# The last group's transition matrix: built transposed, row sums as columns, base blocks put down by TensorE

## The chip, the cores and the metric

One core of one Trainium2 chip. The metric is device microseconds of one execution of the program, the median of 3 runs.

## The reference

128 batches, each with 128 nodes and 512 features, and an adjacency of 128 x 128. Two graph layers, each followed by a residual and a layer norm over the features; cut to what matters:

```python
# layer 0
deg = jnp.sum(adj, axis=-1, keepdims=True)
agg = jnp.einsum('bij,bjf->bif', adj, x) / jnp.maximum(deg, EPS)
x = layernorm(x + relu(jnp.concatenate([x, agg], axis=2) @ W.T))
# layer 1
Xw = X @ Wv + bv
sj = Xw @ aw[:d, 0]
si = Xw @ aw[d:, 0]
e = leaky_relu(sj[:, None, :] + si[:, :, None] + ab[0], negative_slope=0.2)
alpha_matrix = A * jnp.exp(e)
transition = alpha_matrix / (jnp.sum(alpha_matrix, axis=-1, keepdims=True) + 1e-12)
for k in range(3):
    H = H + Xk @ Wk[k] + bk[k]
    Xk = jnp.einsum('bij,bjd->bid', transition, Xk)
x = layernorm(x + relu(H))
```

The part that the change touches is `transition` of the last four batches, and how the sum over k is then put together for them.

## The kernel before

The batches go in 32 groups of four (`G = 4`, `NG = 32`), through layer 0 first and then through layer 1. All numbers are float32; a product is two passes of TensorE. The weight products are done block by block with seven products instead of eight, at two levels. In layer 1 an outer block is one of O1 to O7 (`outer`), each made of seven products of 385 columns, O1.1 to O1.7. Four times 385 columns hold, in this order, X W2, X W1, X W0, two columns for the scores si and sj, and two of padding. So the sum of the reference is taken from the inside, T(T(X W2) + X W1) + X W0 plus biases.

`combine` does that, in eight products of 512 columns (c.1 to c.8; x.1 to x.8 for the last group). For each of the four batches b, `one(b)` multiplies the transition matrix with X W2 into a PSUM bank, VectorE adds X W1 to give `v1`, and ScalarE then copies the base, X W0, into the same bank (`row(b, 254, 766, 1)`). `two(b)` multiplies the transition matrix with `v1` and adds it to what stands in the bank. `residual` follows on VectorE.

The transition matrix comes as follows. `t_scores` takes the score columns out of two of the O results. For all groups but the last, sj goes through memory to be spread over the partitions, the matrix is normed, stored, and loaded back in blocks of 32 (`load_blocks`, by `swap_in`), which VectorE's 32 x 32 transpose then turns (`t_turn`), since TensorE wants it transposed. Most of that lies beside the next group's products. The last group has no next one. There, `t_scores` makes four diagonal matrices of sj (`dg`), and a product with ones spreads them over the partitions (`t_exp`). ScalarE adds si in a leaky ReLU (Prelu) and takes Exp. GpSimd multiplies with the adjacency, VectorE sums the rows and takes the reciprocal (`t_sums`). ScalarE scales the rows, four products with the identity turn the matrix, and ScalarE copies the four results out of PSUM (`t_norm`).

Two lanes of four PSUM banks each (bA0 to bA3, bB0 to bB3) carry the products of two outer blocks side by side. In the last group O4 and the combine stand in lane 1 (bA); lane 0 (bB) is done after O3. At the program's start one identity product is written into each of the eight banks.

The order of the work is written out by hand. `PL` is the order of TensorE's products in the last group, and `PLACES_L` and `PLACES_M` say at which place in it every other operation is issued (`PLACES_M` those of the group before, "group 30", whose layer norm falls into this stage; the last is group 31). Each engine runs its instructions in the order of issue. SyncE issues the transfers, also in order. `late` holds residuals and evictions that are issued right after a product. `need` only checks the order while the program is built.

The names that the steps of the prediction use: c is the combine of group 30; the "early" addition is GpSimd's at L667, the O3.5 addition VectorE's at L670, evictions with an addition L663; L255, L784 are VectorE's transposes; L471 and L967 are additions at the start; L500 is the square whose sum gives the variance; "apply" is the last step of a layer norm (`ln_apply`, `end_apply`); w2row is a small matrix at the start that is turned by products of two columns.

Of the kernel before, what the change touches and what calls it, by code (L numbers as in the profile page):

```python
# [16 lines left out]
def kernel(  # L17
# [15 lines left out]
    P = 128  # L33
# [63 lines left out]
    def load_adj(n):  # L97
        g = n % NG
        adjs[n] = p1.tile([P, G, N], FP, name="ag")
        nc.sync.dma_start(adjs[n], adj[g * G : (g + 1) * G].rearrange("b i j -> i b j"))  # L100
# [46 lines left out]
    for t in bA + bB:  # L147
        nc.tensor.matmul(t, ident, ident[:, None, :].to_broadcast([P, Q, P]), start=True, stop=True)
# [566 lines left out]
    def t_scores(g):  # L715
        need(("O3", g, 7), ("sum_c", g, 0), ("sum_c", g, 1))
        si = small.tile([P, G], FP, name="si")
        for p, t in ((0, rs[NG + g]), (1, last22[g])):
            L_.copy(sj[:, 2 * p : 2 * p + 2], t[:, :, 1, 381])
            L_.activation(si[:, 2 * p : 2 * p + 2], t[:, :, 1, 382], AF.Identity, bias=cc)  # L720
        if g == NG - 1:
            dg = p1.tile([P, G, N], FP, name="dg", tag="sb")
            for b in range(G):
                V.tensor_scalar(dg[:, b], ident, sj[:, b : b + 1], None, ALU.mult)
            Ts[g] = dg, si
            return
        turned = small.tile([P, R], FP, name="turned")
        V.transpose(turned, sj)
        d = dram.tile([R, Q, R], FP, name="scd")
        nc.sync.dma_start(d.rearrange("b q r -> q b r"), turned)  # L730
        Ts[g] = d, si

# [8 lines left out]
    def t_exp(g):  # L741
        need(("t_load", g) if g < NG - 1 else ("t_scores", g))
        T, si = Ts[g]
        if g == NG - 1:
            dg, T = T, p1.tile([P, G, N], FP, name="T", tag="aT")
            pt = lanes[0][0]
            mm(pt, ones[:].to_broadcast([P, P]), dg, True)
        for b in range(G):
            src = T[:, b] if g < NG - 1 else pt[:, b * N : (b + 1) * N]
            L_.activation(T[:, b], src, AF.Prelu, bias=si[:, b : b + 1], alpha=SLOPE)  # L750
        Ts[g] = T, si
        L_.activation(T, T, AF.Exp)
# [12 lines left out]
    def t_norm(g):  # L765
        need(("t_sums", g))
        T, rr = Ts[g]
        for b in range(G):
            L_.activation(T[:, b], T[:, b], AF.Copy, scale=rr[:, b : b + 1])
        if g < NG - 1:  # L770
            swap_out(NG + g, T)
            return
        TTs[g] = p1.tile([P, G, N], FP, name="TT")
        for b in range(G):
            pt = lanes[0][1 + b // 2]
            mm(pt[:, b % 2 * N : (b % 2 + 1) * N], T[:, b], ident, b % 2 == 0)
            L_.copy(TTs[g][:, b], pt[:, b % 2 * N : (b % 2 + 1) * N])
# [8 lines left out]
    def combine(lane, g):  # L786
        n = NG + g
        X, Y, W, Z = lane
        at_ = {0: X, 1: Z, 2: W, 3: Y}
# [8 lines left out]
        def one(b):  # L798
            need(("O4" if b > 1 else "O3", g, 7), ("sum_c", g, 0), ("sum_c", g, 1))
# [4 lines left out]
            L_.copy(at_[b], row(b, 254, 766, 1))  # L804

        def two(b):
            mm(at_[b], TTs[g][:, b], v1[b])
            late.append((residual, n, b, at_[b]))
# [15 lines left out]
    def step(lane, name, g, k):  # L824
# [11 lines left out]
    PL = ("o3.7 O1.1 O1.2 O2.1 O1.3 O2.2 O1.4 O1.5 O1.6 O1.7 O2.3 O2.4 O5.1 O2.5 O2.6 O5.2 O2.7 O5.3 O5.4 O6.1 O5.5 O5.6 "  # L836
          "O6.2 O5.7 O6.3 O7.1 O6.4 O6.5 O7.2 O7.3 O7.4 O6.6 O7.5 O6.7 O7.6 O7.7 O3.1 O3.2 O3.3 O3.4 c.1 c.2 c.3 c.4 "
          "O3.5 c.5 c.6 c.7 c.8 O4.1 O3.6 O4.2 O3.7 O4.3 O4.4 O4.5 O4.6 O4.7 x.1 x.2 x.3 x.4 x.5 x.6 x.7 x.8").split()
# [42 lines left out]
    def place_op(n, pos, name, m, *a):  # L881
# [3 lines left out]
        else:  # L885
# [37 lines left out]
        ("ln_mean",): 213, ("ln_var", 1): 224, ("ln_scales",): 226, ("ln_var", 2): 222, ("ln_apply", 0): 234,  # L923
        ("ln_apply", 3): 237, ("ln_apply", 1): 230, ("y_store", 1): 255, ("ln_var", 0): 224, ("y_store", 0): 243,
        ("ln_var", 3): 213, ("ln_apply", 2): 242,
    }
    PLACES_L = {
        ("end_store", 2): 150, ("t_norm",): 115, ("sum_r", 0): 71, ("end_store", 0): 153, ("t_scores",): 105,
        ("sum_r", 1): 71, ("t_exp",): 107, ("end_apply", 0): 147, ("load_adj",): 96, ("end_apply", 1): 152,
        ("load_y", 1): 94, ("end_store", 1): 163, ("t_sums",): 111, ("end_stats", 3): 137, ("end_mean", 0): 125,  # L930
        ("end_apply", 2): 139, ("end_var", 1): 131, ("end_mean", 1): 130, ("end_stats", 2): 130, ("end_rstd", 2): 132,
        ("load_y", 0): 57, ("end_store", 3): 155, ("end_apply", 3): 151, ("end_scales",): 133, ("end_var", 0): 125,
        ("sum_c", 0): 76, ("end_rstd", 3): 145, ("sum_c", 1): 76,
    }
    OPS = {f.__name__: f for f in (load_left, load_y, load_adj, x_turn, x_inner, x_s1, x_s2, x_s3, x_s4, sum_c22, degree, a_norm, a_load, a_turn, w_slot, ln_mean, ln_var, ln_scales, ln_apply, y_store, sum_r, sum_c, t_scores, t_load,
           t_exp, t_sums, t_norm, t_back, t_turn)}
    ENDS = {f.__name__: f for f in (end_mean, end_var, end_scales, end_stats, end_rstd, end_apply, end_store)}
    LAST = {"ln_mean", "ln_var", "ln_scales", "ln_apply", "y_store"}
    OWN = {"sum_r", "sum_c", "t_scores", "t_load", "t_exp", "t_sums", "t_norm", "t_back", "t_turn"}
# [112 lines left out]
```

## Time and profile before

| | |
|---|---|
| median of 3 runs | 2092.91 us (2092.64 to 2092.97) |
| the profiled execution | 2093.66 us |
| its span, first to last instruction | 2091.9 us |
| mean granted clock of TensorE | 0.998 |
| TensorE products | 2074.7 us, 99% |
| VectorE, ScalarE, GpSimd | 70%, 55%, 73% |

The span is what the trace shows; 1.76 us of the profiled execution lie around it. A time such as 2066.00 is counted from the span's start. In a timeline the first number is the start, the second the duration, then come engine, line, operation, what is written from what, the count, and in brackets how long the engine was idle before it and what ended that. SPq is SyncE's queue. Rows that follow each other are merged.

### The profile page before, as it was taken

The page shows a single profiled execution, that of the slowest core. Times are in us where ns is not written, and L with a number is a line of the kernel's source. Part 1 is how long each engine was busy: PE and PEld are TensorE (multiplying, and loading weights), DVE is VectorE, ACT ScalarE, POOL GpSimd, SP SyncE. Part 2 cuts the span into 40 slices and gives each one's busy share as a digit, 9 for nine tenths or more (in the row PEclk, how much of TensorE's full clock was granted, in tenths as well). Part 3 has the DMA queues.
Part 4 walks back from the last instruction along what each step waited for, and adds up shares of the span by engine and source line. Part 5 has one row for each costly group of instructions (what it writes and reads, how often), then busy time and mean ns, then how long its engine had stood idle before and what let it go on. Part 6 is the DMA issues. An engine that isn't in the chain of part 4 may idle for free.

```text
span 2091.9 us, 25884 instructions
## 1 busy us (share of the span) xinstructions
PE 2074.7 (99%) x7100; PEld 1330.3 (64%) x7100; DVE 1465.5 (70%) x3247; ACT 1153.7 (55%) x2883; POOL 1532.2 (73%) x1424
## 2 busy tenths in 40 slices
PE   9999999999999999999999999999999999999997
PEld 6778888888778886555555555555555555555553
DVE  6777777777777777666666666666666666666665
ACT  2656666666666666355455455455455455455454
POOL 5777888887767776867767767767767767767763
PEclk9999999999999999999999999999999999999999
DMA  9777766676667767335534434534534534534523
GB/s 207 171 189 194 180 178 178 161 190 194 158 165 190 188 171 237 87 86 122 115 87 122 115 86 122 115 86 122 115 86 124 114 86 124 113 87 122 115 66 116
DMA packets 429486, 287.13 MB, mean 137 GB/s; under 512 B 153497, under 2 KB 352281, under 8 KB 429340
## 3 DMA queue, kind: packets, MB, share of 16 engines
q1 hardware_dynamic: 428412, 284.15, 53.7%
q10 hardware_dynamic: 800, 1.31, 0.3%
q8 instruction: 56, 0.92, 0.2%
q14 instruction: 90, 0.74, 0.1%
q0 software_dynamic: 128, 0.01, 0.0%
HBM read 191.60 MB, written 93.79 MB: 136 GB/s over the span
## 4 chain that ended last, share of the span: by engine, by line
PE 96%; DMA 1%; POOL 1%; DVE 1%; ACT 0%; issue 0%; ACTq 0%; DVEq 0%; POOLq 0%
PE bA L151 50%; PE bB L151 45%; DMA big<-in_w0t_dram 1%; DMA yd<-y 0%; DMA xb<-in_x_dram 0%; DMA y<-in_x_dram 0%; PE bA L177 0%; POOL s L667 0%; POOL c L711 0%; POOL r L703 0%; ACT junk L500 0%; DVE y L376 0%; POOL xs L266 0%; POOL xs L270 0%; POOL xu L278 0%
## 5 line engine op out<-in xcount | busy, mean ns | idle before, releaser
L151 PE MATMUL bB<-big,xu 128*128 128x385 f32 (+1 forms) x1806 | 562.1, 434 | 0.7 <-DVE r L670 0.5
L151 PEld LDWEIGHTS bB<-big,xu 128*128 128x128 f32 x1806 | 341.8, 190 | 167.7 <-issue 44.8
L151 PE MATMUL bA<-big,xl 128*128 128x256 f32 (+1 forms) x1358 | 405.8, 416 | 0.4 <-DVE bA L471 0.3
L151 PE MATMUL bB<-big,xs 128*128 128x256 f32 (+1 forms) x1316 | 384.1, 416 | 0.0
L151 PEld LDWEIGHTS bA<-big,xl 128*128 128x128 f32 x1358 | 257.1, 190 | 100.1 <-issue 15.6
L151 PEld LDWEIGHTS bB<-big,xs 128*128 128x128 f32 x1316 | 249.1, 190 | 84.8 <-ACT bB L624 6.2
L151 PE MATMUL bA<-big,xu 128*128 128x256 f32 (+1 forms) x896 | 294.3, 440 | 0.4 <-DVE bA L633 0.2
L667 POOL TENSOR_TENSOR s<-s,r 128x385 f32<-128x385 f32 x128 | 128.1, 1001 | 182.2 <-DVE bB L633 139.1
L151 PE MATMUL bA<-c,TT 128*128 128x512 f32 x512 | 241.3, 593 | 0.0
L500 ACT ACTIVATE junk<-y,mv 128x512 bf16<-128x512 f32 x252 | 182.6, 725 | 89.5 <-POOL mv L495 85.3
L151 PEld LDWEIGHTS bA<-big,xu 128*128 128x128 f32 x896 | 162.0, 189 | 95.4 <-DVE r L657 19.3
L513 ACT ACTIVATE y<-y,mv,rstd 128x512 f32<-128x512 f32 x252 | 202.1, 815 | 0.6 <-POOL mv L508 0.6
L376 DVE SCALAR_TENSOR_TENSOR y<-bA,y 128x512 f32<-128x512 f32 x256 | 170.5, 684 | 23.4 <-PE bA L151 16.9
L151 PE MATMUL bA<-big,xs 128*128 128x385 f32 x448 | 173.7, 499 | 0.0
L151 PE MATMUL bB<-big,xl 128*128 128x385 f32 (+1 forms) x462 | 172.0, 480 | 0.8 <-ACT bA L452 0.4
L633 DVE TENSOR_TENSOR bB<-bB,s 128x385 f32<-128x385 f32 x128 | 72.5, 567 | 121.0 <-PE bB L151 83.2
L151 PEld LDWEIGHTS bA<-c,TT 128*128 128x128 f32 x512 | 97.2, 190 | 89.4 <-issue 48.8
L624 ACT COPY bB<-bB 128x385 f32<-128x385 f32 x128 | 60.1, 470 | 143.8 <-PE bB L151 143.8
L278 POOL TENSOR_TENSOR xu<-xu,xs 128x896 f32<-128x896 f32 x63 | 131.7, 2090 | 8.8 <-PE bB L151 8.8
L274 POOL TENSOR_TENSOR xl<-xu,xl 128x896 f32<-128x896 f32 x63 | 133.5, 2120 | 1.1
L270 POOL TENSOR_TENSOR xs<-xs,xu 128x896 f32<-128x896 f32 x63 | 132.0, 2095 | 2.4
L266 POOL TENSOR_TENSOR xs<-xl 128x896 f32<-128x896 f32 x63 | 131.3, 2085 | 0.0
(182 smaller groups left out, 3474.8 us busy)
## 6 DMA issues: line engine op xcount, KB each, us to landing
xb<-in_x_dram SPq DMA_DIRECT2D x256, 128.0 KB, 3.8
y<-in_x_dram SPq DMA_DIRECT2D x64, 512.0 KB, 4.2
yd<-y SPq DMA_DIRECT2D x64, 512.0 KB, 3.0
xb<-yd SPq DMA_DIRECT2D x256, 128.0 KB, 5.2
y<-yd SPq DMA_DIRECT2D x64, 512.0 KB, 4.6
out_dram<-y SPq DMA_DIRECT2D x62, 512.0 KB, 2.8
ag<-in_adj_dram SPq DMA_DIRECT2D x64, 256.0 KB, 5.1
sb<-sd SPq DMA_DIRECT2D x252, 64.0 KB, 3.2
```

Source lines behind the costliest of these rows:

```text
L151: nc.tensor.matmul(dst, lhsT, rhs, start=start, stop=True, skip_group_check=True)
L266: S_.tensor_add(xs[n][:, 0], xl[n][:, 0], xl[n][:, 1])
L270: S_.tensor_sub(xs[n][:, 1], xs[n][:, 0], xu[n][:, 0])
L274: S_.tensor_sub(xl[n][:, 0], xu[n][:, 0], xl[n][:, 0])
L278: S_.tensor_sub(xu[n][:, 1], xu[n][:, 1], xs[n][:, 1])
L376: V.scalar_tensor_tensor(y, t, 0.0, y, ALU.max, ALU.add, accum_out=mvs[n][:, b, 0:1])
L500: L_.activation(junk, ys[n, b // 2][:, b % 2], AF.Square, bias=mvs[n][:, b, 0:1], accum_out=mvs[n][:, b, 1:2])
L513: L_.activation(y, y, AF.Identity, bias=mvs[n][:, b, 0:1], scale=rstds[n][:, b : b + 1])
L624: L_.copy(Y, X)
L633: V.tensor_add(W, X, s5)
L667: S_.tensor_add(s5, s5, part(src, BZ, BW))
```

## The change

Only the last group and the program's start are changed.

- The matrix is built transposed from the beginning. The diagonals are made of si, and sj is the column that ScalarE adds (`end_scores`); Prelu and Exp go in two halves of two batches. The last group's adjacency is loaded in blocks of 32 and turned by VectorE (`adj_turn`), and VectorE multiplies with it (`end_rows`) in place of GpSimd.
- The row sums are four products with a column of ones, one column each (`end_rows`). VectorE adds epsilon, takes the reciprocal, and makes diagonals of it (`end_recip`). A product with ones spreads these over the partitions, and VectorE multiplies the matrix with that out of PSUM (`end_norm`). The four turning products and their four copies are gone.
- The base of batches 0, 1 and 2 is written by a product with the identity into three banks of lane 0 (`end_base`), and `two(b)` adds to it there. Batch 3 still has its base copied by ScalarE, into bank X.
- `PL`, `PLACES_L` and `PLACES_M` are new: c.5 to c.8 stand together, O4.4 comes before the product that spreads the scores, `sum_c` and O3's early addition change places on GpSimd, the last group's two y loads stand at other places on SyncE, and the last steps of the layer norms have new places.
- The identity product into bank bB3 at the start is left out.

```diff
     def load_adj(n):
         g = n % NG
+        if n == 2 * NG - 1:
+            adjs[n] = p1.tile([P, G, Q, R], FP, name="agb", tag="ag")
+            load_blocks(adjs[n], adj[g * G : (g + 1) * G])
+            return
...
-    for t in bA + bB:
+    for t in bA + bB[:3]:
         nc.tensor.matmul(t, ident, ident[:, None, :].to_broadcast([P, Q, P]), start=True, stop=True)
...
             for b in range(G):
-                V.tensor_scalar(dg[:, b], ident, sj[:, b : b + 1], None, ALU.mult)
+                V.tensor_scalar(dg[:, b], ident, si[:, b : b + 1], None, ALU.mult)
...
+    def adj_turn():
+        need(("load_adj", 2 * NG - 1))
+        src = adjs[2 * NG - 1]
+        adjs[2 * NG - 1] = p1.tile([P, G, N], FP, name="agT", tag="aT")
+        V.transpose(adjs[2 * NG - 1].rearrange("p g n -> p (g n)"), src.rearrange("p g j r -> p (g j r)"))
+
+    def end_scores(g):
+        need(("t_scores", g), ("C", g - 1, 8))
+        (dg, _), pt = Ts[g], lanes[0][0]
+        mm(pt, ones[:].to_broadcast([P, P]), dg, True)
+        T = TTs[g] = p1.tile([P, G, N], FP, name="TT")
+        for b in range(G):
+            L_.activation(T[:, b], pt[:, b * N : (b + 1) * N], AF.Prelu, bias=sj[:, b : b + 1], alpha=SLOPE)
+            if b % 2:
+                L_.activation(T[:, b - 1 : b + 1], T[:, b - 1 : b + 1], AF.Exp)
+
+    def end_rows(g, h):
+        need(("end_scores", g), ("adj_turn",), *[("end_rows", g, 0)] * h)
+        T, pt = TTs[g], lanes[0][0]
+        t2 = T[:, 2 * h : 2 * h + 2].rearrange("p b n -> p (b n)")
+        V.tensor_mul(t2, t2, adjs[2 * NG - 1][:, 2 * h : 2 * h + 2].rearrange("p b n -> p (b n)"))
+        for b in (2 * h, 2 * h + 1):
+            mm(pt[:, b : b + 1], T[:, b], ones, b == 0)
+
+    def end_recip(g, h):
+        need(("end_rows", g, 1))
+        t = lanes[0][0][:, 2 * h : 2 * h + 2]
+        rr = small.tile([P, 2], FP, name="rr2")
+        V.tensor_scalar(rr, t, ROW_EPS, None, ALU.add)
+        V.reciprocal(rr, rr)
+        if h == 0:
+            ends["dr"] = p1.tile([P, G, N], FP, name="dr", tag="sb")
+        for b in (0, 1):
+            V.tensor_scalar(ends["dr"][:, 2 * h + b], ident, rr[:, b : b + 1], None, ALU.mult)
+
+    def end_norm(g, h):
+        need(("end_recip", g, 1), *[("end_norm", g, 0)] * h)
+        T = TTs[g][:, 2 * h : 2 * h + 2].rearrange("p b n -> p (b n)")
+        pt = lanes[0][0][:, h * FH : (h + 1) * FH]
+        mm(pt, ones[:].to_broadcast([P, P]), ends["dr"][:, 2 * h : 2 * h + 2].rearrange("p b n -> p (b n)"), h == 0)
+        V.tensor_mul(T, T, pt)
+
+    def end_base(g, b):
+        need(("sum_c" if b > 1 else "O3", g, 0 if b > 1 else 7))
+        t = (rs[NG + g], last22[g])[b // 2][:, b % 2].rearrange("p n m -> p (n m)")
+        mm(lanes[0][1 + b], ident, t[:, 254:766], True)
...
-        TTs[g] = p1.tile([P, G, N], FP, name="TT")
-        for b in range(G):
-            pt = lanes[0][1 + b // 2]
-            mm(pt[:, b % 2 * N : (b % 2 + 1) * N], T[:, b], ident, b % 2 == 0)
-            L_.copy(TTs[g][:, b], pt[:, b % 2 * N : (b % 2 + 1) * N])
...
-        at_ = {0: X, 1: Z, 2: W, 3: Y}
+        at_ = to = {0: X, 1: Z, 2: W, 3: Y}
+        if g == NG - 1:
+            to = {0: lanes[0][1], 1: lanes[0][2], 2: lanes[0][3], 3: X}
...
-            L_.copy(at_[b], row(b, 254, 766, 1))
+            if g < NG - 1 or b == 3:
+                L_.copy(to[b], row(b, 254, 766, 1))
 
         def two(b):
-            mm(at_[b], TTs[g][:, b], v1[b])
-            late.append((residual, n, b, at_[b]))
+            need(*[("end_base", g, b)] if g == NG - 1 and b < 3 else [])
+            mm(to[b], TTs[g][:, b], v1[b])
+            late.append((residual, n, b, to[b]))
...
     PL = (...)
-          "... O3.1 O3.2 O3.3 O3.4 c.1 c.2 c.3 c.4 "
-          "O3.5 c.5 c.6 c.7 c.8 O4.1 O3.6 O4.2 O3.7 O4.3 O4.4 O4.5 O4.6 O4.7 x.1 x.2 x.3 x.4 x.5 x.6 x.7 x.8")
+          "... O3.1 O3.2 O3.3 O3.4 c.1 c.2 c.3 c.4 "
+          "c.5 c.6 c.7 c.8 O4.1 O3.5 O4.2 O3.6 O3.7 O4.3 O4.4 O4.5 O4.6 O4.7 x.1 x.2 x.3 x.4 x.5 x.6 x.7 x.8")
...
     PLACES_L = {
...
-        ("t_norm",): 115, ("t_scores",): 105, ("t_exp",): 107, ("t_sums",): 111, ("load_adj",): 96, ("load_y", 1): 94, ("load_y", 0): 57,
+        ("t_scores",): 105, ("adj_turn",): 100, ("end_scores",): 108, ("end_base", 2): 110, ("end_base", 0): 111,
+        ("end_rows", 0): 111, ("end_rows", 1): 111, ("end_recip", 0): 111, ("end_recip", 1): 112, ("end_base", 1): 112,
+        ("end_norm", 0): 113, ("end_norm", 1): 115, ("load_adj",): 92, ("load_y", 0): 39, ("load_y", 1): 115,
...
     }
```

In the order of TensorE's queue the end of the changed program is: O4.3, O4.4, the product that spreads the scores, O4.5, base 2, base 0, the four row sums, O4.6, base 1, first norm product, O4.7, second norm product, combine.

## The prediction

> **What bounds the kernel now.** I read the shares of busy time first, then the chain that ended last, then the waits of TensorE, and last the timeline of the two ends.
>
> ```profile
> PE 2074.7 (99%) x7100; PEld 1330.3 (64%) x7100; DVE 1465.5 (70%) x3247; ACT 1153.7 (55%) x2883; POOL 1532.2 (73%) x1424
> ...
> PE 96%; DMA 1%; POOL 1%; DVE 1%; ACT 0%; issue 0%; ACTq 0%; DVEq 0%; POOLq 0%
> ```
>
> TensorE is busy 2074.7 of 2091.9 us: only 17.2 us can be saved without taking a product away. 2.7 of them lie before its first instruction and 8.4 behind its last. The waits of TensorE from 2000 us on show the others:
>
> ```profile
> PE bB L151 <- ACT T L769: 2.2, 1, 2.2
> PE bB L151 <- ACT TT L777: 0.9, 2, 0.5
> PE bB L151 <- DVE dg L724: 0.8, 1, 0.8
> ```
>
> All three are the last group's transition matrix, which nothing covers once the O4 products run out. Its timeline (TensorE alone), and then three two-microsecond stretches (length, busy us and count of PE, PEld, DVE, ACT and POOL, then the granted clock, DMA share, GB/s):
>
> ```profile
> 2054.13 2.74 PE L151 MATMUL bA<-c,TT 128*128 128x512 f32 x6
> ...
> 2066.00 1.12 PE L151 MATMUL bB<-dg,ones 128*128 128x512 f32 x2 [0.79 <-DVE dg L724]
> 2066.97 3.09 PE L151 MATMUL bA<-big,xl 128*128 128x385 f32 x8
> 2072.29 0.49 PE L151 MATMUL bB<-ident,T 128*128 128x128 f32 x2 [2.23 <-ACT T L769]
> ...
> 2075.41 3.46 PE L151 MATMUL bA<-c,TT 128*128 128x512 f32 x6
> ```
>
> ```profile
> 2064.00:2066.00 2.00, 1.22 (x4) 0.38 (x2) 1.39 (x6) 1.01 (x5) 0.00 (x0) 1.00 0.00 0
> ...
> 2074.00:2076.00 2.00, 1.64 (x6) 1.10 (x5) 0.00 (x0) 0.80 (x3) 0.00 (x0) 0.50 0.00 0
> 2076.00:2078.00 2.00, 2.00 (x5) 0.87 (x4) 0.76 (x2) 0.00 (x0) 0.00 (x0) 0.79 0.00 0
> ```
>
> The reader is to see two losses: TensorE waits, and the three products that took 2.74 us in the group before take 3.46 us here, at half the clock. The head of the program:
>
> ```profile
> 2.66 6.52 PE L148 MATMUL bA<-ident 128*128 128x512 f32 x8 [2.66 <-POOL ident masks.py:199]
> ...
> 9.02 3.60 PE L148 MATMUL bB<-ident 128*128 128x512 f32 x8
> ...
> 12.45 3.83 PE L151 MATMUL bA<-big,xu 128*128 128x256 f32 x17
> ```
>
> The eight identity products (two passes each) run until the first real product at 12.45, without a gap. Their weight loads stand 0.85 apart up to 8.6 us and 0.43 after it: the clock is up long before they end.
>
> **The change, part by part.** All times below are on the clock of this trace. A product of 512 columns takes 0.86 us (2.74 for three, less the tail of the last), of 385 columns 0.65.
>
> *One identity product less.* At full clock a product of 512 takes 0.86, so the first real one can start at 11.59. What it reads is there: xu is turned by 9.75, and VectorE uses the same weights at 11.38; their first difference, which the second product needs at 12.45 now, is done at 12.07. The limit is the second x block: VectorE turns it at 15.65 without a wait, its last load was issued at 10.53, and a load on SyncE that waits for this one goes out at 15.43. If it lands only then, the turning moves up by 0.25, the 0.30 us wait behind it (before L471) gives 0.3 more, and the products that follow move by 0.55; if it lands by 14.8, all 0.86 is kept. I take 0.7 (ends 0.5 and 0.86). Behind it TensorE is busy throughout, so a shift reaches the end; the two gaps of the head (0.28 at 26.8, 0.45 at 37) end on VectorE and ScalarE work that moves along.
>
> *The regrouped order of the last group.* The same O1 to O7 products, in another order: 0, at most 0.3 either way (a bubble of one dependent addition). The combine of the group before (c.5 to c.8) now runs without O3.5 between. Its last product waits for VectorE's two additions (0.43, 0.41) and ScalarE's copy (0.59), which start 0.65 earlier like it: 0.1 lost, as now. So O4.3 still ends at 2065.06.
>
> *O4.4 ahead of the broadcast product* fills 0.65 of the 0.79 us wait. The diagonal stays due at 2065.94: VectorE gets the transpose of the adjacency (0.70, row of L784) into the hole between the O3.5 addition (ends 2063.2) and O3.6's, which waits for TensorE until 2063.95. ScalarE has one square ahead of the scores (0.72 and 0.19), and the second pair of si is there at 2065.3, where the third diagonal needs it at 2065.46.
>
> *From the broadcast product to the combine.* Product at 2066.00 to 2066.97. TensorE then goes O4.5 (to 2067.62), base 2 (2068.48), base 0 (2069.34). Beside it ScalarE does two Prelu (from 2067.23, 0.28 apart), Exp of 256 (0.63 for 512 and a copy's 0.47 for 385 against 0.59 for 512: about 0.42), again two and one: 2068.27 and 2069.22. VectorE multiplies 256 columns in 0.42 each (L243): 2068.73 and 2069.68. The four row sums are eight weight loads with one column each; eight such passes (w2row) took from 55.7 to 56.5, so 0.11 each: to 2070.28. Then O4.6 (2070.93), base 1 (2071.79). VectorE meanwhile: plus epsilon 0.18 from 2070.48, reciprocal 0.18, two diagonals (0.28, 0.19 apart; they also wait for a square on ScalarE, whose buffer they take, at 2070.8), O4.6's addition 0.56, the second plus epsilon, which ends at 2071.97. The first norm product must wait for that, since it overwrites the sums: 2072.14, 0.35 idle. It takes 0.43; O4.7 to 2073.22; the second norm waits for VectorE's multiplication of the first half (2072.77 to 2073.20): 2073.37 to 2073.80, 0.15 idle. The combine starts at 2073.80, against 2075.41. Cross-check, O4 products aside: between 2066.97 and 2075.41 stood 5.85 us of waits, transposes and copies; now there are three bases (2.58), two norms (0.86), row sums (0.9) and 0.50 of waits, 4.84; with the 0.65 of O4.4 that is 1.66, against 1.61.
>
> *The combine* is eight products of 0.86 = 6.89, to 2080.68. Before: 2075.41 to 2083.33, which is 7.92. ScalarE's three base copies (0.59 each) are off its path; the fourth is done near 2078.6, due 2079.8. 2.65 us gained at TensorE's end.
>
> *The finish.* VectorE now has apply 2 ahead of the statistics of block 3. Last residual near 2082.3, apply 2 waits for GpSimd's power (0.57) until 2082.63, statistics of block 3 to 2083.98, GpSimd to 2084.88, apply 3 to 2085.46; ScalarE's two applies end at 2085.52 (2087.90 before). The last store goes out at about 2085.95, against 2088.3. That gives back 0.25: tail gain 2.4.
>
> *Hidden moves.* A square of group 30 waits for the second norm, whose diagonals stand in its buffer, to 2074.0; behind it on ScalarE are group 30's applies, from about 2076.5 (2078.56 before). GpSimd loses the 1.27 us multiplication; its early addition for O3.5 ends 1.75 later, at 2057.9, due 2062.7. On SyncE the first y load (512 KB) of the last group moves ahead of the reload of the group before's transition matrix, which landed 2.2 us after issue (by 2048.9) and is needed by VectorE at 2051.99. At the 396 GB/s of that window 512 KB are 1.3 us, so it stays covered; beyond 3 us it would delay c.1. The other y load goes behind the adjacency, due only at 2080. Of lane 0's banks all are free by 2066.
>
> *Two rules weighed.* Row: the clock went to 0.50 after a wait of 2.23, and stayed 1.00 after 0.79. [...] The trace decides: the longest gap becomes 0.35, so I keep 1.00 and the 0.72. Second: the adjacency now comes in 128-byte pieces. The trace's reload in the same form (64 KB each) lands in 2.2 us, the plain adjacency in 6.0 (longest 6.5). [...] By the rows it lands by 2059, four ahead of its transpose at 2063.2. [...] I take the reload's row: 0.
>
> **Sum.** 2.4 + 0.7 = 3.1 us. The profiled execution was 2093.66, span 2091.9 and 1.76 around it; it becomes about 2090.5. The median shown, 2092.91, is 0.75 lower; it becomes 2089.8.
>
> **The rivals.** *More than I count:* head 0.86, the two idles (0.5) not there, a bubble less in the regrouped order (0.3), the finish not slower (0.25): 0.16 + 0.5 + 0.3 + 0.25 on top of 3.1 is 4.3, so 2088.6. For it: a group lasts 39.22 us (the chain's rows at 1957.07 and 1996.29), its 49 and 8 products 38.6, so bubbles are there to win. Against: the norms hang on seven small VectorE steps in a line. *Half of it lost:* x block late (head 0.5), and each of the seven small steps dearer by 0.2, so that the combine starts 1.4 later: 1.5, so 2091.4. *The other side: the clock.* From 2069.3 to 2072.6 TensorE runs single columns, a gap and short products. [...] the half clock falls on the norms and the combine. It decides above 6.2 us of half clock, each costing half of itself. If it lasts to the end, norms, O4.7 and combine (8.4 us) double: 2092.9 + 8.4 - 3.1 = 2098.2. Against: the trace's own half clock lasted some 3.4 us after a far emptier stretch. *The head does nothing* if loads bound it: 2090.5, inside the range.
>
> **Numbers.** Forecast 0.68, more 0.20, half 0.09, clock 0.03. 0.2% is 4.2 us, about what a measurement of this kernel can tell from no change. The forecast and the half case lie within it (0.77), the first rival beyond (0.20), the clock slower (0.03). The range reaches from the first rival's middle and the bounds of head and finish, 2088.3, to the half case, 2091.4.
>
> **What would show it.** Right: first real product near 11.6; no wait over 0.5 us on TensorE after 2060; PEclk 1.00 up to the last product; combine's first three products in 2.74; TensorE's last product about 3.4 earlier, last store about 3.1 earlier. Wrong: a wait on the adjacency's load before its transpose, c.1 waiting for the reload, PEclk 0.50 in the last 15 us, or a first norm product more than 1 us after base 1.

## The result, and the profile after

The changed kernel takes 2089.65 us (median of 20 runs, 2089.05 to 2090.42), the kernel before 2093.03 beside it (20 runs, 2092.07 to 2094.03): ratio 0.9984, 95% interval 0.9977 to 0.9990, so 3.4 us less. The forecast was 2089.8. The sum came out right; two of its terms did not, and they offset each other, which was luck.

The page of the changed kernel, shares of busy time and then the chain that ended last by engine:

```profile
PE 2073.8 (99%) x7108; PEld 1330.4 (64%) x7108; DVE 1467.4 (70%) x3258; ACT 1147.0 (55%) x2872; POOL 1531.1 (73%) x1423
...
PE 96%; POOL 1%; DMA 1%; DVE 1%; issue 0%; ACT 0%; ACTq 0%; SPq 0%; DVEq 0%; POOLq 0%
```

TensorE is busy 2073.8 of a span of 2087.7; the span has lost 4.2 us and the busy time 0.9, so mostly idle time went. After 1990 us the waits of TensorE are an empty list. Its timeline in the last group (the product line is L155 now):

```profile
2052.46 2.74 PE L155 MATMUL bA<-c,TT 128*128 128x512 f32 x6
...
2064.32 1.12 PE L155 MATMUL bB<-dg,ones 128*128 128x512 f32 x2
2065.28 0.81 PE L155 MATMUL bA<-big,xl 128*128 128x385 f32 x2
2065.93 1.02 PE L155 MATMUL bB<-s,ident 128*128 128x512 f32 x2
2066.79 1.02 PE L155 MATMUL bB<-r,ident 128*128 128x512 f32 x2
2067.65 1.05 PE L155 MATMUL bB<-ones,TT 128*128 128x1 f32 x8
2068.56 0.89 PE L155 MATMUL bA<-big,xl 128*128 128x385 f32 x2
2069.29 1.02 PE L155 MATMUL bB<-r,ident 128*128 128x512 f32 x2
2070.28 0.70 PE L155 MATMUL bB<-dr,ones 128*128 128x256 f32 x2
2070.81 0.81 PE L155 MATMUL bA<-big,xl 128*128 128x385 f32 x2
2071.49 0.70 PE L155 MATMUL bB<-dr,ones 128*128 128x256 f32 x2
2072.02 2.74 PE L155 MATMUL bA<-c,TT 128*128 128x512 f32 x6
```

No row carries an idle time in brackets: none of the three former waits is left, and the steps of VectorE and ScalarE run beside O4 products, base products and row sums. The last combine's first three products take 2.74 and not 3.46. Stretches of two microseconds (length, busy us and count of PE, PEld, DVE, ACT, POOL, then granted clock, DMA share, GB/s) show the same from the other side, TensorE full and the clock at 1.00:

```profile
2068.00:2070.00 2.00, 2.00 (x10) 1.19 (x9) 1.16 (x6) 1.10 (x4) 0.00 (x0) 1.00 0.00 0
2070.00:2072.00 2.00, 2.00 (x7) 1.16 (x7) 1.63 (x7) 0.00 (x0) 0.00 (x0) 1.00 0.00 0
2072.00:2074.00 2.00, 2.00 (x6) 0.95 (x5) 1.45 (x5) 0.81 (x2) 0.73 (x2) 1.00 0.00 0
2074.00:2076.00 2.00, 2.00 (x6) 0.87 (x5) 1.79 (x5) 1.19 (x2) 0.69 (x2) 1.00 0.00 0
```

The head, all engines:

```profile
2.66 5.70 PE L152 MATMUL bA<-ident 128*128 128x512 f32 x8 [2.66 <-POOL ident masks.py:199]
...
8.20 2.74 PE L152 MATMUL bB<-ident 128*128 128x512 f32 x6
...
10.77 1.03 PE L155 MATMUL bA<-big,xu 128*128 128x256 f32 x4
...
12.16 4.58 PE L155 MATMUL bA<-big,xu 128*128 128x256 f32 x20 [0.36 <-DVE big L1013]
...
15.44 0.71 DVE L259 STREAM_TRANSPOSE xl<-xb 128x512 f32<-128x512 f32 x1 [0.74 <-DMA xb<-in_x_dram]
...
16.86 0.73 PEld L155 LDWEIGHTS bA<-big,xl 128*128 128x128 f32 x4 [0.52 <-DVE bA L475]
```

The first real product starts 1.68 earlier, at 10.77, but TensorE then waits for VectorE's weight difference, VectorE waits 0.74 for the second x block, and the first lower-half product (bA<-big,xl; its weight load is the last row) starts at 16.86 against 17.63.

To compare two traces, three points serve. The first combine product (c,TT) of the program stands at 41.60 before and 40.99 after; the first of the last but one combine at 2054.13 and 2052.46; the last store's issue ends at 2088.70 and 2084.64. The profiled executions (2093.66 and 2089.45) thus differ by 0.61 in the head; 0.80 from there to 2015.21 (2013.80 after), where the program is the same; 0.26 in the reordered O1 to O7; 2.39 in the tail; 0.14 behind the last store. That is 4.20 of 4.21. The 0.80 is not the change's: from the c,TT product at about 41 us to the one at about 1505 the first profiles took 1463.65 (before) and 1463.02 (after), and a second profile of each took 1463.07 (before) and 1463.58 (after). Below, "tail" is the time from the first c,TT product of the last but one combine to the end of the last store's issue: 34.57 before, 32.18 after.

### The profile page after: what moved, and what is told of

Same layout as the page of the kernel before. It is cut to its first block, busy times and chain, and to the rows that moved or that the text cites. A ratio compares the mean times of both kernels' runs of the same rounds, so it can differ in the third digit from the quotient of the medians.

```text
span 2087.7 us, 25906 instructions
## 1 busy us (share of the span) xinstructions
PE 2073.8 (99%) x7108; PEld 1330.4 (64%) x7108; DVE 1467.4 (70%) x3258; ACT 1147.0 (55%) x2872; POOL 1531.1 (73%) x1423
## 4 chain that ended last, share of the span: by engine, by line
PE 96%; POOL 1%; DMA 1%; DVE 1%; issue 0%; ACT 0%; ACTq 0%; SPq 0%; DVEq 0%; POOLq 0%
PE bA L155 50%; PE bB L155 46%; DMA xb<-in_x_dram 0%; DMA yd<-y 0%; DMA big<-in_w0t_dram 0%; DMA y<-in_x_dram 0%; PE bA L181 0%; POOL s L671 0%; POOL c L715 0%; POOL r L707 0%; POOL xs L270 0%; POOL xs L274 0%; POOL xu L282 0%; DVE y L380 0%; ACT y L517 0%
## 5 line engine op out<-in xcount | busy, mean ns | idle before, releaser
L155 PE MATMUL bB<-big,xu 128*128 128x385 f32 (+1 forms) x1806 | 561.6, 433 | 0.6 <-DVE r L674 0.5
L155 PEld LDWEIGHTS bB<-big,xu 128*128 128x128 f32 x1806 | 341.9, 190 | 167.1 <-issue 44.4
L155 PE MATMUL bA<-big,xl 128*128 128x256 f32 (+1 forms) x1358 | 406.2, 416 | 0.4 <-DVE bA L475 0.3
L155 PE MATMUL bB<-big,xs 128*128 128x256 f32 (+1 forms) x1316 | 384.1, 416 | 0.0
L155 PEld LDWEIGHTS bA<-big,xl 128*128 128x128 f32 x1358 | 257.0, 190 | 99.9 <-issue 15.3
L155 PEld LDWEIGHTS bB<-big,xs 128*128 128x128 f32 x1316 | 249.1, 190 | 84.7 <-ACT bB L628 5.9
L155 PE MATMUL bA<-big,xu 128*128 128x256 f32 (+1 forms) x896 | 294.3, 440 | 0.7 <-DVE big L1013 0.4
L155 PE MATMUL bA<-c,TT 128*128 128x512 f32 x512 | 240.6, 592 | 0.0
L155 PEld LDWEIGHTS bA<-big,xu 128*128 128x128 f32 x896 | 161.8, 189 | 95.6 <-DVE r L661 19.2
L155 PE MATMUL bA<-big,xs 128*128 128x385 f32 x448 | 173.5, 499 | 0.0
L155 PE MATMUL bB<-big,xl 128*128 128x385 f32 (+1 forms) x462 | 172.0, 480 | 0.8 <-ACT bA L456 0.4
L155 PEld LDWEIGHTS bA<-c,TT 128*128 128x128 f32 x512 | 96.9, 189 | 89.2 <-issue 48.9
```

The source lines that it names most:

```text
L155: nc.tensor.matmul(dst, lhsT, rhs, start=start, stop=True, skip_group_check=True)
```

## The experiments

Theory at first: the gain is 2.4 us of tail, up to 0.7 of head and 0.3 of order. Rival: the head does nothing and the tail is worth more than the shown profile says.

| kernel | median, us | before beside it | ratio, 95% interval | half clock in the tail, us | last combine starts | tail |
|---|---|---|---|---|---|---|
| before, first and second profile | – | – | – | 3.41; 6.83 | 21.28; 21.29 | 34.57; 36.15 |
| changed, first and second profile | 2089.65; 2089.56 | 2093.03; 2092.92 | 0.9984 (0.9977 to 0.9990); 0.9983 (0.9977 to 0.9990) | 0; 0 | 19.56; 19.57 | 32.18; 32.19 |
| head alone | 2093.14 | 2093.19 | 1.0000 (0.9992 to 1.0008) | 6.83 | 21.47 | 35.60 |
| changed, eight identity products | 2089.76 | 2093.19 | 0.9983 (0.9977 to 0.9990) | 0 | 19.57 | 32.18 |
| changed, old order of O1 to O7 | 2089.59 | 2093.19 | 0.9983 (0.9976 to 0.9990) | 0 | 19.56 | 32.17 |
| changed, four identity products | 2089.51 | 2093.19 | 0.9984 (0.9977 to 0.9990) | 0 | 19.57 | 32.18 |
| before, wait filled | 2091.41 | 2093.60 | 0.9990 (0.9981 to 0.9998) | 0 | 20.56 | 33.12 |
| changed, bases by ScalarE | 2092.39 | 2093.60 | 0.9995 (0.9987 to 1.0003) | 6.83 | 21.92 | 35.24 |
| the same with filler | 2090.24 | 2092.92 | 0.9987 (0.9980 to 0.9993) | 0 | 19.57 | 32.53 |
| changed, O4.4 behind | 2090.49 | 2093.60 | 0.9985 (0.9978 to 0.9991) | 0 | 20.11 | 32.73 |
| changed, finish reordered | 2089.48 | 2093.60 | 0.9980 (0.9973 to 0.9987) | 0 | 19.57 | 31.42 |
| the same, epsilon on VectorE | 2089.09 | 2092.92 | 0.9980 (0.9973 to 0.9988) | 0 | 19.57 | 31.28 |

"Last combine starts" and "tail" count from the first c,TT product of the last but one combine. "Half clock" is read from the granted clock; for the four-identity kernel it is that of the tail, its head is told below.

**The head alone.**

```diff
 # before
-    for t in bA + bB:
+    for t in bA + bB[:3]:
```

> The kernel before with seven identity products ahead of the first real one, and nothing else of the change. Theory (the shift that the head gives reaches the end whole, and the change's trace showed 0.61 us of it at 41 us): 0.6 us less than before, so a ratio near 0.9997; the first lower-half product (bA<-big,xl) starts at 16.9 and not 17.6, because the second x block lands at about 15.4 and is then the limit, and the first c,TT product at 41.0 and not 41.6. The last group's tail stays as it was: last store ends 34.6 after the first c,TT product of the last but one combine. Rival (the head does nothing, its start only wandered between two executions): ratio 1.0000, c,TT at 41.6. Rival (the head holds more than counted, since the change's medians fell by 3.4): 0.9995 or lower.

The trace did what the theory said (lower half at 16.97, c,TT at 41.10), and the time did not: 2093.14 against 2093.19 (the interval is wide enough, though, to hold the expected 0.6). Its last store still ends at 2088.68, because the tail of this execution is 35.60 long. TensorE around the old wait, and the stretches beside it:

```profile
2071.23 0.80 PE L151 MATMUL bB<-ident,T 128*128 128x128 f32 x2 [2.23 <-ACT T L769]
...
2074.55 4.39 PE L151 MATMUL bA<-c,TT 128*128 128x512 f32 x6
```

```profile
2072.00:2074.00 2.00, 1.29 (x6) 0.97 (x5) 0.00 (x0) 0.85 (x4) 0.05 (x1) 0.50 0.00 0
2074.00:2076.00 2.00, 2.00 (x4) 1.23 (x5) 0.00 (x0) 0.27 (x1) 0.00 (x0) 0.50 0.00 0
2076.00:2078.00 2.00, 2.00 (x4) 0.75 (x3) 0.76 (x2) 0.65 (x2) 0.00 (x0) 0.53 0.00 0
```

The wait is the same 2.23, but the half clock lasts from 2071.04 to 2077.87, not 3.41 as in the profile that the prediction read: the first three products take 4.39, not 3.46. The tail of the kernel before is not one number.

**The changed kernel without its head.**

```diff
 # changed
-    for t in bA + bB[:3]:
+    for t in bA + bB:
```

> The changed kernel with the eighth identity product put back. Theory: 0.6 us more than the changed kernel, 2.7 us less than before (2.4 of the tail, 0.3 of the new order of O1 to O7), ratio 0.9987; from the first c,TT product of the last but one combine to the end of the last store 32.2 us, as in the changed kernel. The first lower-half product starts at 17.6 if the clock rises at 8.6 us as in the profile of before, but near 16.9 if it rises at 7 as in that of after, because then the second x block is the limit with eight products too. Rival (the head is worth more and the tail less): the time stands over 1 us above the changed kernel's.

2089.76: 0.1 to 0.2 above the changed kernel (2089.65 and 2089.56), not 0.6. Here the clock came up early (the weight loads go from 0.85 to 0.43 apart between 6.2 and 6.9 us), the eight identity products give way to the first real one at 11.57, and the limit is the same as with seven:

```profile
15.38 0.71 DVE L259 STREAM_TRANSPOSE xl<-xb 128x512 f32<-128x512 f32 x1 [0.52 <-DMA xb<-in_x_dram]
...
16.80 0.73 PEld L155 LDWEIGHTS bA<-big,xl 128*128 128x128 f32 x4 [0.29 <-DVE bA L475]
```

**The old order of O1 to O7 in the changed kernel.**

```diff
-    PL = ("O1.1 o3.7 O1.2 O1.3 O2.1 O2.2 ... O3.4 c.1 c.2 c.3 c.4 "   # changed
+    PL = ("o3.7 O1.1 O1.2 O2.1 O1.3 O2.2 ... O3.4 c.1 c.2 c.3 c.4 "   # as before
```

> The changed kernel with the old order of O1 to O7 and of the combine products c.1 to c.4 in the last group; the new order begins behind c.4. Theory (the prediction said 0, at most 0.3 either way; the two traces differ by a bubble of 0.3 between 2026 and 2036): 0.3 us more than the changed kernel, and 38.92 us again, not 38.66, from the last but two combine's first product (2015.21 before) to the last but one's (2054.13 before); the tail behind it 32.2 to the last store, as in the changed kernel. Rival (the order was needed by the tail, because something in it comes later without it): the tail lengthens by over 0.5. Rival (only a difference between executions): 38.66 stays.

In the trace the stretch is 38.92 again (2013.84 to 2052.76), so the 0.26 belongs to the order; the tail behind it is unchanged. The times (2089.59) do not resolve so little.

**Four identity products in place of seven.**

```diff
-    for t in bA + bB[:3]:
+    for t in bA[1:3] + bB[1:3]:
```

> The changed kernel with four identity products in place of seven. Theory (since the change, VectorE's differences and the second x block set the head, not the identity products): the first real product waits for xu and starts at 10.3, the next waits for VectorE's weight difference to 12.2 as in the changed kernel, the first lower-half product at 16.8 to 16.9: no gain, ratio to before as for the changed kernel, 0.9985. Rival (each identity product less is worth 0.43 to 0.86): 1.3 to 2.6 us less than the changed kernel. Rival (TensorE needs them to come to full clock): the clock rises later or falls back in the hole between the identity products and 12.2, and the lower-half products come over 0.5 later than 16.9.

2089.51, no gain and no loss that the times resolve. The profiled execution was the slowest of its 21 (2091.26): its first real products waited for weights, and then the half clock came back for 3.41 us.

```profile
9.46 0.70 PE L155 MATMUL bA<-big,xu 128*128 128x256 f32 x2 [1.70 <-DMA big<-in_w0t_dram]
10.95 0.67 PE L155 MATMUL bA<-big,xu 128*128 128x256 f32 x2 [0.79 <-DMA big<-in_w0t_dram]
12.37 6.24 PE L155 MATMUL bA<-big,xu 128*128 128x256 f32 x20 [0.75 <-DVE big L1013]
18.45 0.81 PE L155 MATMUL bA<-big,xl 128*128 128x256 f32 x3
```

Four of the 21 runs lie at 2090.67 to 2091.26 and all others at 2089.86 or less, so most executions seem to escape this; only the profiled one shows its cause.

**The old tail with its wait filled.** Products that nobody reads stand where TensorE waited for T.

```diff
 # before, t_norm of the last group, ahead of the transposes
+        for w in (4, 4, 2):
+            mm(lanes[0][3][:, : w * P], ident, ident[:, None, :].to_broadcast([P, w, P]), True)
```

> The kernel before with filler in its longest late wait: behind O4.7 of the last group TensorE multiplies the identity by itself into a bank that nothing reads (512, 512 and 256 columns, 2.14 us at full clock, where TensorE waited 2.23 us for T), and nothing else is changed. Theory (the wait brings the clock down; how long it stays down differs between executions, 3.4 us in the profile of before, 6.1 us in that of the kernel with seven identity products, so the shown profile was a mild one): PEclk stays 1.00 to the last product, the last combine takes 6.9 us and not 7.9 or more, the last store ends 33.3 after the first c,TT product of the last but one combine (before 34.6, with seven identity products 35.6), and the median falls by 1.8 (1.2 to 2.3), ratio 0.9991. Rival (the profile of before shows the usual cost): 1.0 to 1.2 less. Rival (the half clock has another cause than the wait): no change. The rest to the changed kernel, some 1.6 us, is then the earlier start of the combine.

2.2 us less with useless products alone (ratio 0.9990, 0.9981 to 0.9998), and all but one of the 13 runs lie within 2090.94 to 2091.57, where those of the kernel before reach from 2092.48 to 2095.36. The transposes run at full clock and the combine is back to 2.74:

```profile
2068.58 2.31 PE L151 MATMUL bB<-ident 128*128 128x512 f32 x6
2070.97 0.49 PE L151 MATMUL bB<-ident,T 128*128 128x128 f32 x2
...
2073.39 2.74 PE L151 MATMUL bA<-c,TT 128*128 128x512 f32 x6
```

The tail is 33.12. With 3.41 us of half clock it was 34.57, with 6.83 it was 35.60 and 36.15: so the short one costs about 1.5, the long one 2.5 to 3.0, and the 2.2 of the medians lies between. What is left to the changed kernel is 0.94 of tail.

**The base blocks by ScalarE in the changed kernel.** The three base products go; what they filled becomes waiting.

```diff
 # changed
-        if g == NG - 1:
-            to = {0: lanes[0][1], 1: lanes[0][2], 2: lanes[0][3], 3: X}
...
-            if g < NG - 1 or b == 3:
-                L_.copy(to[b], row(b, 254, 766, 1))
+            L_.copy(to[b], row(b, 254, 766, 1))
...
-            need(*[("end_base", g, b)] if g == NG - 1 and b < 3 else [])
# and the three ("end_base", b) places are taken out
```

> The changed kernel without the three identity products for the base blocks: ScalarE copies the base blocks into the combine's own banks, as the kernel before did. Theory (the norms wait for VectorE's chain, so the base products only fill waits): the combine starts as in the changed kernel, 19.6 (19.4 to 19.8) after the first c,TT product of the last but one combine, with TensorE idle for 1.2 before the row sums, 0.5 in them and 0.9 before the first norm; time within 0.3 of the changed kernel if the clock stays at 1.00. Rival (the base products are on the path): 0.9 to 2.6 us less. Rival (these waits are enough to bring the clock down): PEclk 0.50 in the combine, 1.5 to 3 us more than the changed kernel.

The second rival happened. The waits came as worked out, and they brought the clock down, from 2068.20 to 2075.03:

```profile
2067.20 0.58 PE L155 MATMUL bB<-ones,TT 128*128 128x1 f32 x4 [1.14 <-ACT TT L750]
2068.05 0.91 PE L155 MATMUL bB<-ones,TT 128*128 128x1 f32 x4 [0.28 <-DVE TT L758]
2068.82 1.63 PE L155 MATMUL bA<-big,xl 128*128 128x385 f32 x2
2071.17 1.22 PE L155 MATMUL bB<-dr,ones 128*128 128x256 f32 x2 [0.72 <-DVE rr L766]
```

An O4 product pair takes 1.63 there, and 0.89 in the changed kernel. Most of the gain is gone: the median is 1.2 us below that of before, with an interval (0.9987 to 1.0003) that does not exclude no gain at all, and the runs spread from 2090.6 to 2093.65, as the kernel before does.

**The same, with filler in place of the base products.**

```diff
 # the kernel above, with the places of end_base put back
-        mm(lanes[0][1 + b], ident, t[:, 254:766], True)
+        mm(lanes[0][1 + b], ident, ident[:, None, :].to_broadcast([P, Q, P]), True)
```

> As the kernel in which ScalarE copies the base blocks, but with three products of the identity by itself, into banks that nothing reads, where the changed kernel has its three base products. Theory (what the base products bring is that TensorE has no wait there, and so keeps its clock; as arithmetic ScalarE's copies do as well): PEclk 1.00 to the last product, the combine starts 19.6 after the first c,TT product of the last but one combine, the last store ends 32.2 to 32.5 after it, time within 0.3 of the changed kernel, and 2.4 to 3 less than without the filler. Rival (the fall of the clock came from ScalarE's copies or the products' order, not from the waits): 35 again. Rival (the copies stand on the combine's path): 0.6 to 1.2 more than the changed kernel at full clock.

The clock stays at 1.00 and the combine starts at 19.57, as in the changed kernel:

```profile
2066.70 1.88 PE L155 MATMUL bB<-ident 128*128 128x512 f32 x4
2068.42 1.05 PE L155 MATMUL bB<-ones,TT 128*128 128x1 f32 x8
2069.34 0.89 PE L155 MATMUL bA<-big,xl 128*128 128x385 f32 x2
2070.07 1.02 PE L155 MATMUL bB<-ident 128*128 128x512 f32 x2
...
2072.80 2.74 PE L155 MATMUL bA<-c,TT 128*128 128x512 f32 x6
```

So the waits brought the clock down, and not ScalarE's copies, which are the same in both. What is left is 0.68 by the medians (2090.24 against 2089.56 on the same chip): the copies do cost, as the last rival said. In the traces 0.29 arises in the combine (its last product ends 26.88 after the reference product, 26.59 in the changed kernel), 0.05 in the rest of the tail, and 0.38 behind the last store: ScalarE, busy with copies, scales the group before later, its store goes out 1.36 later, close ahead of the four last ones, and these land in 2.7 and not 2.3 us (median). That the one makes the other is likely, but was not tried alone.

**O4.4 behind the broadcast product.**

```diff
-        ... ("end_scores",): 108
+        ... ("end_scores",): 107
```

> The changed kernel with the broadcast product of the scores ahead of O4.4, as before. Theory (O4.4 fills 0.65 of the wait for the diagonal, and all behind it hangs on ScalarE and VectorE in a line that starts at the broadcast product): the broadcast product starts where it did, 11.9 after the first c,TT product of the last but one combine, behind a wait of 0.6 to 0.8; O4.4 falls behind it and the combine starts 0.65 later, so 0.65 more than the changed kernel. Rival (the norms' chain sets the start of the combine, and a product more behind the broadcast product only fills a wait there): no change, within 0.2.

The wait for the diagonal is back, and the combine starts 0.55 later (20.11), of which all reaches the last store (32.73). The median is 3.1 us below that of before on its chip, against 3.4 for the changed kernel, which the intervals do not tell apart. No fall of the clock:

```profile
2064.80 1.13 PE L155 MATMUL bB<-dg,ones 128*128 128x512 f32 x2 [0.79 <-DVE dg L728]
```

**The finish in another order, and then with less on GpSimd.**

```diff
 # changed
-        ("end_apply", 2): 133, ("end_scales",): 134, ("end_apply", 0): 147, ("end_store", 0): 148
+        ("end_apply", 2): 137, ("end_scales",): 132, ("end_apply", 0): 145, ("end_store", 0): 146
```

> The changed kernel with another order in the finish: VectorE takes the statistics of block 3 ahead of the scaling of block 2, GpSimd the power for blocks 0 and 1 ahead of that for block 2, and the store of block 0 goes out first. Theory (the end hangs on GpSimd's powers in a row, 0.6 to 0.8 each, and ScalarE's two scalings start 0.9 earlier): ScalarE's scalings end near 2082.9 and not 2083.8, VectorE's last near 2083.4 and not 2083.7, the last store goes out 0.3 to 0.4 earlier: 0.3 less than the changed kernel. Rival (the stores' own issue, 0.8 each on SyncE, sets the end once they follow each other): no gain.

```diff
 # on top of that
-        S_.tensor_scalar(ve, ends[b][:, 1:2], 1.0, LN_EPS, ALU.mult, ALU.add)
+        V.tensor_scalar(ve, ends[b][:, 1:2], LN_EPS, None, ALU.add)
-        ("end_apply", 2): 137
+        ("end_apply", 2): 140
```

> The changed kernel with the reordered finish, and with the addition of epsilon for blocks 2 and 3 on VectorE instead of GpSimd. Theory (GpSimd's row of small operations sets the end: the reordered finish ended its last store 31.4 after the first c,TT product of the last but one combine, against 32.2; each addition taken from GpSimd shortens that row by 0.19 and its hop of 0.09): last store 30.9 to 31.2 after that product, 1.0 to 1.3 us less than the changed kernel on the same chip, ratio to before 0.9979. Rival (the stores' issue sets the end by now): 31.4 again, 0.7 less than the changed kernel.

The tail shrinks by 0.76 in the first (31.42), twice what was expected, and by only 0.14 more in the second (31.28, between the theory's 31.2 and the rival's 31.4); the median of the second is 2089.09, 0.47 below the changed kernel on the same chip: faster than both kernels, at less than half of what was expected. In the trace the last store's issue ends 0.91 earlier, but the time from there to the end of the span grows from 3.06 (second profile of the changed kernel) to 3.43. The issues of the stores, the changed kernel's first profile ahead of the last kernel's (KB each, median us to landing):

```profile
out_dram<-y SPq DMA_DIRECT2D x4, 256.0 KB, 2.3
```

```profile
out_dram<-y SPq DMA_DIRECT2D x4, 256.0 KB, 2.5
```

The four last stores now go out within 1.84 us and not 3.2, and take longer to land. So the rival, that the stores set the end, is half true.

**Both kernels once more.**

> The changed kernel itself once more, so that the two kernels below have it on the same chip, and to see where the clock comes up in its head a second time. Theory (the change's gain is the clock in the tail, 2.2 us, and the earlier combine, about 1, and the head gives nothing): 3.4 us less than before, ratio 0.9984; the clock stays at 1.00 from 20 us to the last product; from the first c,TT product of the last but one combine to the end of the last store 32.2. Rival (the tail differs between executions of the changed kernel too, as it does in the kernel before): 32.2 is missed by over 0.5.

> The kernel before itself once more, for one look at its clock. Theory (the moment at which the clock rises in the head and falls in the tail is not tied to the program, and differs between executions): the identity products reach full clock at another time than 8.6 us, the first lower-half product starts between 16.8 and 17.6, the half clock of the tail lasts between 3 and 6.5 us, and the last store ends 34.3 to 36 after the first c,TT product of the last but one combine. Rival (both are fixed by the program): 8.6, 17.6, 3.4 and 34.6 again.

The changed kernel repeats its tail to 0.01 (32.19), although its clock came up at another time in the head (between 7.9 and 8.7 us by the weight loads, not between 6.2 and 6.9; first real product at 11.66, not 10.77). The kernel before does not repeat: lower half at 17.06, the half clock 6.83 long, tail 36.15, the last two a little beyond what was expected (6.5 and 36).

```profile
2071.07 0.49 PE L151 MATMUL bB<-ident,T 128*128 128x128 f32 x2 [2.22 <-ACT T L769]
...
2074.22 5.12 PE L151 MATMUL bA<-c,TT 128*128 128x512 f32 x6
```

```profile
2074.00:2076.00 2.00, 2.00 (x5) 0.97 (x5) 0.00 (x0) 0.27 (x1) 0.00 (x0) 0.50 0.00 0
2076.00:2078.00 2.00, 2.00 (x4) 0.94 (x3) 0.87 (x3) 0.98 (x2) 0.00 (x0) 0.50 0.00 0
2078.00:2080.00 2.00, 2.00 (x4) 0.72 (x3) 1.25 (x4) 0.94 (x2) 0.00 (x0) 0.75 0.00 0
```

The same six instructions took 3.46, 4.39 and 5.12 in three executions of the same tail. That is the term that the prediction took from one of them.

## Why the prediction was right, and which of its terms were not

**One identity product less: 0.7, wrong.** Measured is 0.05 by the head alone and 0.1 to 0.2 by putting the product back, both inside the noise; by the traces the first c,TT product stands at 41.2 on average over the four profiles with eight products (41.60, 40.94, 41.09, 41.19) and at 40.9 over the nine with seven (40.63 to 41.10). So 0.1 to 0.3. The step that failed is the base of the sum, "the first real one can start at 11.59" against 12.45, read from one execution. Its clock came up late, at 8.37; with eight products the first real one started at 11.57, 11.94 and 11.82 elsewhere. The limit named in the same paragraph, the second x block, was right, but then it already binds with eight: VectorE waits 0.52 for it in two of the four profiles with eight, and the first lower-half product starts at 16.80 to 17.12 in the other three and at 16.66 to 16.97 with seven (leaving out the one with four), where the profile that was read has 17.63. The rival "the head does nothing" is the nearest case.

**The regrouped order: 0, at most 0.3.** 0.26 in the trace, and back when the order is undone, within the bounds. In both traces with the old order two starts 12.3 and 12.7 us behind the last but two combine's first product come 0.24 and 0.11 late; with the new order that bubble is gone and two of 0.05 stand elsewhere.

**O4.4 ahead of the broadcast product: 0.65.** 0.55. The diagonal's wait with O4.4 in place is gone, as said.

**From the broadcast product to the combine.** Predicted 19.67 after the reference product (2073.80 minus 2054.13), measured 19.56. The row sums took 0.91 for eight passes (predicted 0.9). Of the idle times of 0.35 and 0.15 ahead of the norms next to nothing is left: VectorE's second epsilon ends at 2070.22 and the norm follows at 2070.28, 0.99 after the start of base 1, which takes 0.86.

**The combine at full clock: right in the shown execution, mis-sized for the median.** The end of TensorE moved by 2.77 (predicted 2.65). The finish gave back 0.38 (predicted 0.25). Tail: 2.39, predicted 2.4. But the half clock was priced from one profile, in which it lasted 3.41 us; in two others it lasted 6.83. For the median the filled wait gives 2.2 for the clock, and from its trace to the changed kernel's there are 0.94 of tail and 0.26 of order: 3.4 in all, which is what the medians show. Of the 0.94, two parts were undone alone, O4.4's place (0.55) and the base products (0.35 of tail); what the transposed matrix gives by itself was not run. How often the half clock lasts 3.41 and how often 6.83 is open: with the old wait in place, it was 3.41 in one profile and 6.83 in two. The bound at the start of the prediction, 17.2 us to save "without taking a product away", was too low for the same reason: TensorE's busy time holds products at half clock (three in 3.46 and not 2.74).

**Hidden moves: 0.** Right. The row used for the adjacency in 128-byte pieces was too kind, though: 64 KB took 4.6 us to land (predicted 2.2). Issued by 2051.39, it was still there well ahead of its transpose at 2061.53, which does not wait.

**The two rows weighed.** On the clock, the row was rightly trusted (0.50 after a wait of 2.23, 1.00 after 0.79): with the 2.23 filled, the clock stayed at 1.00. What the prediction missed is how long the half clock lasts. Behind waits of 2.23, 2.22 and 2.23 in the same tail it lasted 3.41 in the first profile of before, and 6.83 in its second and with the head alone, so a single profile is one draw. The fall costs the tail about 1.5 or 2.5 to 3.0, and the prediction's 2.4 of tail holds the short case alone. In the head, full clock began at between 5.5 and 8.6 us in the 14 profiles.

**The rivals.** "The clock" (the sparse stretch of row sums and norms falls to half clock) did not happen in the changed kernel (1.00 from 2064 to 2080), but it can: without the base products the clock was at half from 2068.20 to 2075.03 in the profiled execution, and with useless products in their place it stayed at 1.00. It had been thought of as a matter of the single columns; the same eight single-column passes stand in both, so the products between are what prevents it.

**The sum.** 3.1 was forecast as 2.4 of tail and 0.7 of head; the runs make it about 3.1 of tail (2.2 and 0.94), 0.26 of order and 0.1 to 0.3 of head. That is 3.5 to 3.7 for a measured 3.4. The total was close because the head was counted too high by about as much as tail and order were counted too low, and that was luck: the profile that was read happened to have both a late clock in its head and only 3.41 us of half clock in its tail.

## What to carry to other kernels

A wait of TensorE ahead of a dense stretch can cost more than its length: filling one of 2.23 us with products, even useless ones, was worth 2.2 us here. A change that replaces other engines' copies by products pays in part by keeping TensorE busy: with waits in place of the base products the kernel was 1.2 us below that of before beside it, with useless products 2.7. Where a profile shows a fall of the clock, its length is one draw (3.41 in one profile of a tail, 6.83 in two others): profile the kernel more than once before pricing it, or give both ends. A sparse stretch can be weighed against stretches of the same kernel whose clock is known: here waits of 1.14 and 0.28 close together were followed by half clock, and a single one of 0.79 among full products was not. A gain in the head can end at the next load: look for what lands last there in an execution whose clock came up early.

## What the runs showed of the hardware

- The half clock lasted 3.41 us (2073.43 to 2076.84 in the first profile of before; 12.35 to 15.76 with four identity products) or 6.83 (2072.18 to 2079.00 in the second profile of before, 2071.04 to 2077.87 with the head alone, 2068.20 to 2075.03 with the bases by ScalarE). What decides between the two was not shown.
- In two microseconds that end at these falls or up to 0.4 ahead of them TensorE was busy for 0.60 (first profile of before), 0.49 (its second), 0 (head alone), 0.63 (bases by ScalarE) and 0.83 (four identity products). Two microseconds with 1.15 (in the filled tail), 1.21 (O4.4 behind) and 1.22 (before, at the wait for the diagonal) were not followed by a fall. A wait alone did not settle it: with four identity products, one of 1.70 ended at 9.46 (0.54 busy from 8 to 10), the clock stayed at 1.00, and it fell at 12.35 behind two more waits, of 0.79 and 0.75. How much waiting it takes was not shown.
- The fall with the bases by ScalarE came behind waits of 1.14 and 0.28, with eight single-column passes between and behind. Behind a wait of 0.78 to 0.79 among full products the clock stayed at 1.00 for at least 6 us, in five profiles.
- In the head the column of the granted clock reads 1.00 from the first product on, while the weight loads stand 0.85 apart up to some moment between 5.5 and 8.6 us (another in each of the 14 profiles) and 0.43 after it. The traces hold no clock record ahead of that moment (the first is at 8.37 in the first profile of before), so there the spacing of the rows tells the clock, the column does not.
- An unchanged stream of products took 1463.0 to 1463.7 us in different executions of both kernels and their variants: 0.05% that no change explains, more than some terms of the sum (one and the same kernel twice: 1463.65 and 1463.07).
- GpSimd's power took 0.56 to 0.63 for one column, 0.71 to 0.79 for two and 1.03 to 1.04 for four, so most of it does not grow with the columns. Three in a row set the finish of the changed kernel: VectorE's last scaling waited 0.98 for the third.
